# Transposing x by blocks of 32 by 32 on VectorE, with a load that puts the blocks in their places

## The chip, the cores and the metric

The kernel runs on one core of one Trainium2 chip. The time is the device time of one execution in microseconds; of three runs of the kernel before the median is 3130.37 us (3129.48 to 3130.62). All data are float32. The engines of the core are named by their work: TensorE multiplies matrices and writes PSUM (eight banks), VectorE (DVE in the profile) and ScalarE (ACT) work element by element, GpSimd (POOL) issues the gathers and scatters and some sums, and SyncE (SP) only issues DMAs. PEld in the profile is TensorE's weight load, which runs beside the product before it.

## The reference

Four graph layers are applied in turn to `x` of shape 128 x 128 x 256 (graphs, nodes, features); after each one `x = layernorm(x + layer(x))`. Cut to what matters:

```
# layer 0: attention over 512 given edges (src, dst)
Xq, Xv = x @ W_lin.T, x @ W_val.T                    # the products that this change is about
e    = einsum(leaky_relu(Xq[:, src] + Xq[:, dst]), a) + log(adj[src, dst] + 1e-8)
attn = softmax of e over the edges with one src
y    = segment_sum(attn * Xv[:, dst]) @ W_out.T
# layer 1: three times  h = relu((adj * adj) @ (h @ W)), widths 512, 1024, 256 (the last without relu)
# layer 2: diagonal, upper and lower part of adj, each with its own 256 x 256 weight, and a bias
# layer 3: normalized adj @ x, then linear 512, batch norm, relu, linear 256, batch norm
```

Batch norm in layer 3 needs all graphs before it can go on, so the kernel has a main phase and a last phase.

## The kernel before, in words

Four graphs make a quad; there are 32 quads (`NQ`). The 128 nodes lie on the 128 partitions. In the main phase the function `iteration(k)` handles several quads at once, each in another stage: `g = k + 3` is entered (its query and value products, the spill of the queries, the gathers), `e = k + 2` has its edge scores and softmax, `b = k + 1` its aggregation and the first products of layer 1, `c = k` the rest of layer 1 and layer 2, `a = k - 1` layer 3's first half. The order of the work on each engine is the order in which the code calls it; nothing is reordered by a planner (`tc.manual_schedule`). Each engine goes through its own list in order and waits where an operand is not there yet. `start()` and `iteration_0()` bring the first four quads in by hand; quads 4 to 31 go through `iteration(k)` for k = 1 to 28.

The product of layer 0 needs `x` with the features on the partitions. In `iteration(k)` the entering quad goes this way:

- `load_x(g, "xg", 1, xpool)` (lines 203 to 206, called at 945 and for quad 4 at 1089) loads the quad with nodes on the partitions, one DMA on SyncE's queue. There is one buffer `xg`, so the load for the next quad is issued when the last reader of `xg` is done.
- `values_in(g, xg)` (lines 236 to 248) transposes it: for each pair of graphs four products of TensorE with the identity into one PSUM bank (line 245), and a copy by VectorE to a buffer `xt` (line 247).
- `query_sums(g)` (line 318) calls `node_blocks`, which makes four sums of blocks (lines 181 to 184). They serve a product scheme with seven block products in place of eight (class `Seven`, steps `p1` to `p7`).
- `queries(g, room)` (line 298) is that scheme for the query and value weights side by side; its products are on line 289, the kept parts are copied by ScalarE on line 306, and sums with kept parts are on line 314.
- `spill(g)` (line 265) writes the queries to DRAM through SyncE's queue, and `gather(g)` (GpSimd, line 336) reads them back by edge ends, first three gathers by `src`, then three by `dst` that add. `score(g, 0)` (lines 368 to 371, VectorE) reads the first of them.

The order around the change. The large product of layer 1, `second(c, between)`, has 14 places at which other work is slipped in; place 11 takes the transposes (and before them the start of the softmax of `e`), place 12 two scans of that softmax:

```
between[11].append(lambda: next(steps, None))
if has_g:
    between[11] += [lambda: values_in(g, quads[g].xg), lambda: query_sums(g)]
between[12] += [lambda: next(steps, None)] * 2
```

After `second` come, in this order: the load of the next `xg`, `stage_f(a)` (16 products, line 801, and two copies by ScalarE into `ag`, line 804), and then the steps of the query product `q` mixed with those of `h`, layer 3's first linear product (line 837):

```
stage_f(a)
h = hidden(a, room[5:] + room[2:4])
q.p1()
next(steps, None)
run(q.p5, q.p2, q.p6)
run(h.p1, h.p5)
```

`q.p6` adds to the bank that `q.p1` filled, so it waits until ScalarE has kept that bank (line 306). On ScalarE that copy stands behind the last relu of `second` (line 596, which takes a sum that VectorE makes on line 592) and behind the two copies into `ag`.

SyncE's queue carries in each pass, in this order: the load of `xr` (line 205), the store `x3d` (788), the load of `xg` (205), the spill `qd` (268), the store `zd` (858), the load of the attention weights `ad` (427). `node_blocks` is also called by `first_seven` (line 506) on the tiles `mx`.

Of the kernel before, what the change touches and what calls it, by code (L numbers as in the profile page):

```python
# [8 lines left out]
F32 = mybir.dt.float32  # L9
# [17 lines left out]
def gnn_stack(ctx: ExitStack, tc: tile.TileContext, x, adj, w_qv_t, a, w_out_t, src, dst,  # L27
# [14 lines left out]
    nc = tc.nc  # L42
# [86 lines left out]
    with ExitStack() as phase:  # L129
# [73 lines left out]
        def load_x(q, tag="xr", bufs=3, pool=wk):  # L203
            t = pool.tile([P, QB, D], F32, tag=tag, name=f"{tag}{q}", bufs=bufs)
            nc.sync.dma_start(t, x[q * QB:(q + 1) * QB].rearrange("b n d -> n b d"))
            return t

        quads[0].xr = load_x(0)
        wqv = cload([P, DC, 2 * D], "wqv", w_qv_t.rearrange("(c p) f -> p c f", p=P), pool=xpool)
        a_sb = cload([P, N], "adj", adj)  # L210
# [22 lines left out]
        def temp(name):  # L233
            return wk.tile([P, 512], F32, tag="t", name=name, bufs=6)

        def values_in(k, xg, copy=None):

            copy = copy or nc.vector.tensor_copy
            s = quads[k]
            s.xts = []  # L240
            for j in range(0, QB, 2):
                pt = ps("pt").rearrange("p (b c n) -> p b c n", b=2, c=DC)
                for t in range(2):
                    for c in range(DC):
                        nc.tensor.transpose(pt[:, t, c, :], xg[:, j + t, c * P:(c + 1) * P], ident)
                xt = temp("xt").rearrange("p (b c n) -> p b c n", b=2, c=DC)
                copy(xt, pt)
                s.xts.append(xt)
# [28 lines left out]

        def node_blocks(tiles, room):

            a = {f"A{j + 1}{c + 1}": tiles[j][:, :, c, :] for j in range(2) for c in range(2)}  # L280
            for i in range(4):
                a[f"S{i + 1}"] = room[i // 2][:, (i % 2) * 256:(i % 2 + 1) * 256].rearrange("p (b n) -> p b n", b=2)
            sums_a(a, a)
            return a
# [31 lines left out]
            return Seven(node_product(blocks, queries.blocks), part, out)  # L316

        def query_sums(k):
            quads[k].x_blocks = node_blocks(quads[k].xts, [temp("xs") for _ in range(2)])

        def gather(k):

# [179 lines left out]
        def first_seven(k):  # L502

            s = quads[k]
            room = room_of("adc", 4)
            a = node_blocks([s.mx[0], s.mx[2]], room)

            def part(bank, i):

                to = room[2 + i % 2]  # L510
                nc.scalar.copy(to, bank)
                return to

            def out(row, col, bank, kept_):
                h1 = temp("h1")
                if kept_ is not None:
                    nc.vector.tensor_add(h1, bank, kept_)
                nc.scalar.activation(h1, bank if kept_ is None else h1, AF.Relu)
                for t in range(2):
                    for c in range(2):  # L520
                        s.h1[2 * row + t, 2 * col + c] = h1[:, (2 * t + c) * P:(2 * t + c + 1) * P]

            return Seven(node_product(a, first_seven.blocks), part, out)
# [377 lines left out]
        def iteration(k):  # L901
            a, c, b, e, g = k - 1, k, k + 1, k + 2, k + 3
            has_c, has_b, has_e, has_g = c < NQ, b < NQ, e < NQ, g < NQ
            if has_b and b > 2:
                quads[b].xr = load_x(b)
            if has_c:
                late_sums(c)
            parts = quads[a].layer2
            if not has_c:

                h = quads[a - 1].hidden
                h.p6()
                for _ in range(4):
                    next(parts)
                next(parts)
                h.p7()
                for _ in parts:
                    pass

                def amid():  # L920
                    run(h.p4, h.p3)
                    hidden_stats(a - 1)

                stage_f(a, amid)
                for i in range(K3):
                    hidden_last(a, i)
                return
            steps = softmax_parts(e) if has_e else iter(())
            if has_c:
                between = {i: [] for i in range(14)}  # L930
                for i in (0, 1, 2, 3, 5, 7):
                    between[i].append(lambda: next(parts, None))
                between[11].append(lambda: next(steps, None))
                if has_g:
                    between[11] += [lambda: values_in(g, quads[g].xg), lambda: query_sums(g)]
                between[12] += [lambda: next(steps, None)] * 2
                if has_e:
                    for c_, i in enumerate((0, 2, 4)):
                        between[i].append(lambda c_=c_: score(e, c_ + 1))
                if has_b:  # L940
                    for j, i in enumerate((5, 8, 9, 10)):
                        between[i].append(lambda j=j: by_row(b, j))
                second(c, between)
            if has_g and g + 1 < NQ:
                quads[g + 1].xg = load_x(g + 1, "xg", 1, xpool)
            elif has_g:
                kept["w2t"] = xpool.tile([P, K3, D], F32, tag="xg", name="l3w2", bufs=1)
                nc.sync.dma_start(kept["w2t"], l3_w2_t.rearrange("(c p) f -> p c f", p=P))
            if has_c:
                room = room_of("m2", 7)  # L950
            next(steps, None)
            if has_g:
                q = queries(g, room[:3])
            stage_f(a)
            if not has_b:
                last_sums()
                h = quads[a].hidden = hidden(a, room[5:] + room[3:5])
                for _ in third(c, 0):
                    pass
                rest = third(c, 2)  # L960
                next(rest)
                third_mix(c, 0)
                third_norm(c, 0)
                for _ in rest:
                    pass
                h.p1()
                third_mix(c, 2)
                third_norm(c, 2)
                lower = kept["m2"][:, :3 * 512].rearrange("p (t f) -> p t f", t=2)
                quads[c].layer2 = layer2(c, None, lower)  # L970
                next(quads[c].layer2)
                run(h.p5, h.p2)
                next(quads[c].layer2)
                return
# [9 lines that stand above are left out]
                q.p7()  # L984
            run(h.p2, h.p6)
            next(steps, None)
            if has_g:
                run(q.p4, q.p3)
                spill(g)
            h.p7()  # L990
            if has_b:
                aggregate(b)
            run(h.p4, h.p3)
            hidden_stats(a)
            if has_g:
                gather(g)
            if has_b:
                stage_a(b)
            for _ in third(c, 0):
                pass  # L1000
            if has_e:
                attention(e)
                scatter(e)
            rest = third(c, 2)
            mix1(b, 0)
            mix1(b, 2)
            third_mix(c, 0)
            next(rest)
            w = first_seven(b)
            third_norm(c, 0)  # L1010
            next(rest)
            run(w.p1, w.p5, w.p2)
            next(rest)
            if has_g:
                score(g, 0)
                gather_last(g)
            w.p6()
            next(rest, None)
            w.p7()
            third_mix(c, 2)  # L1020
            w.p4()
            w.p3()
            quads[c].layer2 = layer2(c, b)
            next(quads[c].layer2)
            third_norm(c, 2)
            next(quads[c].layer2)
# [56 lines left out]
        def late_loads():  # L1083
            nc.sync.dma_start(w3_sb, w3.rearrange("(c p) f -> p c f", p=P))
            for c in range(DC):
                nc.sync.dma_start(l2w[:, c, :].rearrange("p (k f) -> p k f", k=3),
                                  l2_w[:, c * P:(c + 1) * P, :].rearrange("k p f -> p k f"))
            nc.sync.dma_start(l3w1, l3_w1_t.rearrange("(c p) f -> p c f", p=P))
            quads[4].xg = load_x(4, "xg", 1, xpool)

        def small_loads():
            nc.sync.dma_start(bias, bass.AP(tensor=l2_bias.tensor, offset=l2_bias.offset, ap=[[0, P], [1, D]]))
# [537 lines left out]
```

## Time and profile before

| what | value |
|---|---|
| median of three runs | 3130.37 us |
| profiled execution | 3130.48 us, its span 3128.8 us |
| granted TensorE clock, mean | 0.997 |
| TensorE transposes of `xg` (L245) | 232, 8 a quad, 272 ns each, started 0.11 us apart |
| VectorE copies of them (L247) | 56, 2 a quad, 681 ns each |
| load of `xg` | 29 DMAs of 512 KB, 0.38 us of issue, 3.8 us to landing (median) |
| one pass of `iteration(k)` | 85.74 us |

The profile is of one execution on the chip, taken by the hardware profiler. Each instruction has a start, a length, the engine, the line of the kernel and the names of the tiles. In the order of time, a bracket tells how long the engine was idle before the instruction and what ended that; no bracket means that it followed on. Matmuls are pipelined: the length shown is from start to end of one, while the next one starts earlier, so what a group takes is read from its start to the start of the next group. Times are counted from the start of the span.

### The profile page before, as it was taken

To read this page: it belongs to the slowest core of one execution; us is meant where nothing else is said; L and a number is where in the kernel's file an instruction comes from. 1 tells how busy PE (TensorE), PEld (TensorE's weight loads), DVE (VectorE), ACT (ScalarE), POOL (GpSimd) and SP (SyncE) were. 2 spreads that over 40 slices of the span, in tenths; PEclk is the share of its full clock that TensorE was granted. 3 is DMA by queue.
4 is the path that set the end of the run, shared out by engine and by line. 5 is a ranking of instruction groups with operands and counts; after the bars stand their busy time and mean duration, and the time that the engine had idled before them with its cause. 6 is when DMAs were issued, how large, how long until landed. Compare 5 with 4: busy or idle time off the path is not lost. (4 is left out here: it accounts for less than half of the span.)

```text
span 3128.8 us, 39836 instructions
## 1 busy us (share of the span) xinstructions
PE 3075.6 (98%) x14800; PEld 2401.8 (77%) x14800; DVE 2316.9 (74%) x4600; ACT 1375.8 (44%) x2548; POOL 652.3 (21%) x536
## 2 busy tenths in 40 slices
PE   8899999999999999999999999999999999999987
PEld 4688888888888888888888888888888887874444
DVE  8777777777777777777777777777777776458888
ACT  3344443444444444434344444444443444326668
POOL 3311112222211111122222211111222220001135
PEclk9999999999999999999999999999999999999999
DMA  5633233333333332333333333323333331005557
GB/s 182 160 102 94 77 94 109 99 104 109 108 102 82 108 96 80 89 108 102 102 109 109 102 89 101 97 78 95 104 102 101 109 108 41 21 27 206 176 193 273
DMA packets 117473, 340.05 MB, mean 109 GB/s; under 512 B 14880, under 2 KB 51616, under 8 KB 108960
## 3 DMA queue, kind: packets, MB, share of 16 engines
q0 software_dynamic: 44688, 148.40, 19.4%
q1 hardware_dynamic: 70832, 188.18, 16.9%
q8 instruction: 118, 1.93, 0.3%
q10 hardware_dynamic: 1760, 0.92, 0.1%
q14 instruction: 75, 0.61, 0.1%
HBM read 252.00 MB, written 85.46 MB: 108 GB/s over the span
## 5 line engine op out<-in xcount | busy, mean ns | idle before, releaser
L580 PE MATMUL ph<-m,w 128*128 128x256 f32 x2048 | 473.1, 379 | 0.0
L660 PE MATMUL p<-w,h 128*128 128x256 f32 x2048 | 462.8, 379 | 0.0
L580 PEld LDWEIGHTS ph<-m,w 128*128 128x128 f32 x2048 | 386.8, 190 | 77.9 <-issue 14.8
L660 PEld LDWEIGHTS p<-w,h 128*128 128x128 f32 x2048 | 388.9, 190 | 66.4 <-issue 7.9
L336 POOL DMA_INDIRECT zs<-qd,src_idx x120 | 116.3, 969 | 1372.6 <-DMA qd<-qt 1338.2
L580 PE MATMUL ph<-m,w_s 128*128 128x256 f32 x1536 | 357.7, 379 | 0.4 <-DVE h L592 0.4
L580 PEld LDWEIGHTS ph<-m,w_s 128*128 128x128 f32 x1536 | 291.7, 190 | 53.6 <-issue 14.8
L336 POOL DMA_INDIRECT zs<-qd,dst_idx x120 | 189.0, 1575 | 332.5 <-DMA zs<-qd,src_idx 323.7
L586 ACT COPY u<-ph 128x512 f32<-128x512 f32 x128 | 74.8, 584 | 354.9 <-PE ph L580 354.9
L418 POOL DMA_INDIRECT attd<-at,att_idx x128 | 141.3, 1104 | 340.3 <-DMA attd<-at,att_idx 252.4
L596 ACT ACTIVATE h<-h 128x512 f32<-128x512 f32 x192 | 121.1, 631 | 138.9 <-DVE h L592 138.9
L113 ACT ACTIVATE ln_sd<-ln_mv,eps 128x2 f32<-128x2 f32 x192 | 55.9, 291 | 276.6 <-DVE ln_mv L108 276.6
L368 DVE SCALAR_TENSOR_TENSOR zs<-zs 128x1024 f32<-128x1024 f32 x125 | 151.4, 1211 | 7.1 <-DMA zs<-qd,dst_idx 5.1
L370 DVE TENSOR_TENSOR zs<-zs,a_bc 128x1024 f32<-128x1024 f32 x125 | 153.1, 1225 | 4.3
L371 DVE TENSOR_REDUCE scores<-zs 128x16 f32<-128x1024 f32 x125 | 152.5, 1220 | 4.3
L723 ACT COPY x2k<-y 128x384 f32<-128x384 f32 x192 | 92.0, 479 | 144.5 <-PE y L716 109.9
L106 DVE BATCH_NORM_STATS2 ln_st<-xr 128x6 f32<-128x256 f32 x384 | 144.6, 419 | 6.6
L121 DVE TENSOR_SCALAR xr<-xr,ln_mv,ln_rs 128x256 f32<-128x256 f32 x384 | 142.8, 414 | 7.0
L592 DVE TENSOR_TENSOR h<-ph,u 128x512 f32<-128x512 f32 x128 | 87.0, 680 | 71.7 <-PE ph L580 54.4
L437 ACT COPY adc<-ad 128x512 f32<-128x512 f32 x125 | 132.9, 1065 | 8.6 <-DMA ad<-attd 8.6
L684 POOL TENSOR_TENSOR xb<-xr,bias 128x512 f32<-128x512 f32 x64 | 99.2, 1549 | 150.7 <-DVE xr L121 143.7
L537 PE MATMUL pm<-wt_t,h 128*128 128x128 f32 x1024 | 126.9, 277 | 0.0
(347 smaller groups left out, 6086.3 us busy)
## 6 DMA issues: line engine op xcount, KB each, us to landing
ad<-attd SPq DMA_DIRECT2D x32, 1024.0 KB, 4.8
zd<-z SPq DMA_DIRECT2D x31, 1024.0 KB, 7.4
zl<-zd SPq DMA_DIRECT2D x62, 512.0 KB, 3.8
xr<-in_x_dram SPq DMA_DIRECT2D x32, 512.0 KB, 7.2
x3d<-xr SPq DMA_DIRECT2D x32, 512.0 KB, 2.6
x3l<-x3d SPq DMA_DIRECT2D x32, 512.0 KB, 5.3
out_dram<-x3l POOLq DMA_DIRECT2D x31, 512.0 KB, 5.7
xg<-in_x_dram SPq DMA_DIRECT2D x29, 512.0 KB, 3.8
```

Source lines behind the costliest of these rows:

```text
L106: nc.vector.bn_stats(st[:, i, :], r[:, i, :])
L121: nc.vector.tensor_scalar(r[:, i, :], r[:, i, :], mv[:, i, 0:1], rs[:, i:i + 1], op0=ALU.subtract, op1=ALU.mult)
L336: nc.gpsimd.indirect_dma_start(out=s.z[c], out_offset=None, in_=s.qd, in_offset=bass.IndirectOffsetOnAxis(ap=idx[:, c:c + 1], axis=0), com ...
L368: nc.vector.scalar_tensor_tensor(z, z, SLOPE, z, op0=ALU.mult, op1=ALU.max)
L370: nc.vector.tensor_mul(z3, z3, a_bc.unsqueeze(1).to_broadcast([P, QB, D]))
L371: nc.vector.reduce_sum(s.es[:, c, :], z.rearrange("p (r d) -> p r d", d=DH), axis=AX.X)
L418: nc.gpsimd.indirect_dma_start(out=ad, out_offset=bass.IndirectOffsetOnAxis(ap=att_idx[:, c:c + 1], axis=0), in_=s.at[:, c, :], in_offset= ...
L437: (copy or nc.scalar.copy)(s.adc[:, j * H:(j + 1) * H, :], s.ad.rearrange("p (s r) -> p r s", r=R)[:, j * H:(j + 1) * H, :])
L537: nc.tensor.matmul(pm[:, c // 2, c % 2, :], quads[k].h1[i, c], wt_t, start=True, stop=True)
L580: nc.tensor.matmul(bank[g][:, i].rearrange("p b n -> p (b n)"), wa[:, c, f:f + P], s.m2[:, blk_b, c].rearrange("p b n -> p (b n)"), start= ...
L596: nc.scalar.activation(h, h if src_ is None else src_, AF.Relu)
L660: nc.tensor.matmul(p3[:, t * D:(t + 1) * D], s.h2[f // 2][:, f % 2, j + t, :], w3_sb[:, f, :], start=(f == 0), stop=(f == K2 - 1))
```

## The change

The load of a quad from 4 on is made by `load_turned`: eight DMAs, one for each block of 32 features, each to 32 partitions. Partition i*32 + n of the tile then holds, for feature block i, the nodes n, 32 + n, 64 + n and 96 + n of the four graphs, 32 features each (128 bytes that lie together in DRAM). A VectorE transpose of every 32 by 32 block in place then leaves the features on the partitions and the nodes along the row, one transpose of 128 x 512 for each half of the features. `values_in` is no longer called for these quads; its products with the identity and its copies out of PSUM go away there. The first four quads are brought in as before. `node_blocks` takes the two halves of the features as separate tiles.

```diff
+        B = 32
+
+        def load_turned(q):
+            t = xpool.tile([P, DC, QB * N], F32, tag="xg", name=f"xg{q}", bufs=1)
+            xq = x[q * QB:(q + 1) * QB].rearrange("b (j n) d -> n (b j) d", n=B)
+            for c in range(DC):
+                for i in range(P // B):
+                    d0 = c * P + i * B
+                    nc.sync.dma_start(t[i * B:(i + 1) * B, c, :].rearrange("p (m d) -> p m d", d=B), xq[:, :, d0:d0 + B])
+            return t
...
         def node_blocks(tiles, room):
-            a = {f"A{j + 1}{c + 1}": tiles[j][:, :, c, :] for j in range(2) for c in range(2)}
+            a = {f"A{j + 1}{c + 1}": tiles[j][c] for j in range(2) for c in range(2)}
...
         def query_sums(k):
-            quads[k].x_blocks = node_blocks(quads[k].xts, [temp("xs") for _ in range(2)])
+            s = quads[k]
+            xt = [temp("xt") for _ in range(DC)]
+            for c in range(DC):
+                nc.vector.transpose(xt[c], s.xg[:, c, :])
+            s.x_blocks = node_blocks([[t[:, j * 256:(j + 1) * 256].rearrange("p (b n) -> p b n", b=2) for t in xt]
+                                      for j in range(2)], [temp("xs") for _ in range(2)])
...
-            a = node_blocks([s.mx[0], s.mx[2]], room)
+            a = node_blocks([[s.mx[j][:, :, c, :] for c in range(DC)] for j in (0, 2)], room)
...
                 if has_g:
-                    between[11] += [lambda: values_in(g, quads[g].xg), lambda: query_sums(g)]
+                    between[11].append(lambda: query_sums(g))
...
-                quads[g + 1].xg = load_x(g + 1, "xg", 1, xpool)
+                quads[g + 1].xg = load_turned(g + 1)
...
-            quads[4].xg = load_x(4, "xg", 1, xpool)
+            quads[4].xg = load_turned(4)
```

## The prediction

> **What bounds the kernel now.** I read the page first (busy shares), then the busy time of each engine over one pass of the steady loop, then in order of time the instructions of TensorE, VectorE and ScalarE around the edited place, the waits, and last the SyncE queue and the DMA rows. The first line is the page's, the second the busy time by stretch (length, then PE, PEld, DVE, ACT, POOL with counts, granted clock, DMA share, GB/s).
>
> ```profile
> PE 3075.6 (98%) x14800; PEld 2401.8 (77%) x14800; DVE 2316.9 (74%) x4600; ACT 1375.8 (44%) x2548; POOL 652.3 (21%) x536
> ...
> 1055.35:1141.09 85.74, 85.74 (x435) 70.63 (x434) 63.67 (x125) 35.80 (x67) 16.86 (x14) 1.00 0.35 99
> ```
>
> One pass takes 85.74 us, TensorE is busy in all of it at the full granted clock, VectorE in 63.67. So a TensorE instruction that goes should shorten the pass, unless something else at that very place is as late as TensorE is. That is the question here, so the order of time (start, length, engine, line):
>
> ```profile
> 1055.24 0.27 PE L385 MATMUL pe<-ident,scores 128*128 128x128 f32 x1
> 1055.35 1.04 PE L245 MATMUL pt<-ident,xg 128*128 128x128 f32 x8
> 1056.23 1.89 PE L580 MATMUL ph<-m,w 128*128 128x256 f32 x8
> ...
> 1063.20 1.03 PE L289 MATMUL x<-wqv,xt 128*128 128x256 f32 x4
> 1064.06 1.11 PE L289 MATMUL y<-wqv_s,xs 128*128 128x256 f32 x4
> 1065.00 1.03 PE L837 MATMUL y<-ag,l3w 128*128 128x256 f32 x4
> ```
>
> ```profile
> 1055.45 0.69 DVE L592 TENSOR_TENSOR h<-ph,u 128x512 f32<-128x512 f32 x1 [1.39 <-PE ph L580]
> 1056.05 1.28 DVE L247 COPY xt<-pt 128x512 f32<-128x512 f32 x2
> 1057.37 0.42 DVE L181 TENSOR_TENSOR xs<-xt 128x256 f32<-128x256 f32 x1
> ...
> 1061.22 0.65 DVE L592 TENSOR_TENSOR h<-ph,u 128x512 f32<-128x512 f32 x1
> ```
>
> ```profile
> 1061.91 0.63 ACT L596 ACTIVATE h<-h 128x512 f32<-128x512 f32 x1 [2.63 <-DVE h L592]
> 1062.44 1.05 ACT L804 COPY ag<-pa 128x512 f32<-128x512 f32 x2
> 1063.38 0.60 ACT L306 COPY m<-y 128x512 f32<-128x512 f32 x1
> ```
>
> ```profile
> PEld y L289 <- ACT m L306: 6.0, 28, 0.2
> ```
>
> The reader is to see a second chain beside TensorE's own. VectorE waits for a product until 1055.45 and then runs with no idle bracket: the sum L592, the two copies of the edit, four node sums, two scans, the next L592, done at 1061.87. ScalarE's relu L596 waits 2.63 us for exactly that; behind it in ScalarE's order stand the two `ag` copies and the copy L306, which ends at 1063.98. Step p6 of the query product (y<-wqv_s,xs at 1064.06) cannot begin before it: the last line says that its weight load waits for L306 in all 28 passes, 0.2 us each, and its group is 1.11 us long where its neighbours are 1.03. So at 1064 the two chains arrive together. TensorE has no slack there, and neither has the way over VectorE and ScalarE.
>
> **The change, part by part.**
>
> *Removed on TensorE.* 8 transposes a quad for quads 4 to 31, 28 quads (the first four still go through the identity). The group starts at 1055.35 and the next at 1056.23; start to start it is 0.873 us in the median of the 28 groups, 24.45 us in all. Sent through in full, this is 3130.48 - 24.45 = 3106.0. But TensorE would be at p6 at 1063.19, while L306 ends at 1063.98: VectorE's start at 1055.45 hangs on a product ahead of the transposes, and none of its work down to L592 was waiting for TensorE. So what is late next is L306, and the 0.87 us becomes a wait before p6. Taken at 0 us, if VectorE's part keeps its length.
>
> *Exchanged on VectorE.* Two copies out of PSUM, 1056.05 to 1057.37, 1.32 us with the step to L181, become two transposes of 128x512. No transpose of VectorE is in the trace. By rows of its other work: two 128x512 operations within SBUF follow each other at 0.72 us when the first is not overlapped (L553 at 1116.73, L554 at 1117.45), so 1.44 us, which is +0.12 us a quad. If the operation goes at half that rate, it is like a 128x1024 row (L368 to L370, 1.25 us apart): 2.50 us, +1.18 us. At a quarter, 5.0 us, +3.7 us. At twice the rate it is like the 128x256 sums, 0.34 to 0.46 us apart: 0.8 us, -0.52 us. I take +0.12, since operations on 512 elements within SBUF (L553, 682 ns) and out of PSUM (L247, 681 ns) agree and are the nearest. Every such difference goes 1:1 through L592, L596, L804 and L306 into p6 and so into the pass, since no engine idles between: 28 x 0.12 = +3.4 us.
>
> The page "VectorE: DVE Perf Modes" of the Trainium skill, section "The three transpose paths", gives 311 ns for a 128x128 transpose in bf16; with 384 more columns at the page's 0.96 GHz an estimate is 711 ns, and the sum would be 3133 instead. The same section warns that a plain DMA with a transposing access pattern is 19 times slower than the crossbar's 1309 ns; were that so here, 8 blocks would take some 199 us a quad and no pass could hide it. Its condition is a large stride of the innermost run at the destination, which these loads do not have; no row of this trace shows such a load.
>
> *Added waits on VectorE.* The transposes read what eight DMAs wrote, four each. The nearest row is L412, which waits for the landings of four scatters with two semaphore instructions of 50 ns a pass. They pass while the operation ahead (L592, 0.69 us) still runs: 0 us; without that cover 4 x 0.05 us, 28 x 0.2 = 5.6 us. Queued behind are the node sums, the scans and L592. The node sums read 256 elements as before, 0 us.
>
> *The load.* One DMA of 512 KB (512 runs of 1 KB) becomes eight, with 4096 runs of 128 bytes.
>
> ```profile
> 1056.42 0.38 SPq L205 DMA_DIRECT2D xg<-in_x_dram  x1
> 1071.00 0.32 SPq L268 DMA_DIRECT2D qd<-qt  x1
> ...
> L1095 SPq DMA_DIRECT2D bn<-in_l_g_dram x2: 868/951/1034, 116.1 to 118.7; - x2
> ```
>
> ```profile
> 1058.50:1059.00 0.50, 0.50 (x4) 0.45 (x3) 0.50 (x3) 0.50 (x2) 0.00 (x0) 1.00 1.08 385
> ...
> 121.75:122.25 0.50, 0.50 (x5) 0.42 (x4) 0.00 (x0) 0.41 (x1) 0.50 (x1) 1.00 0.38 3
> ```
>
> In the first stretch only xg moves: 385 GB/s for 0.5 us are 188 runs of 1 KB, 1.08 x 16 x 0.5 us of engine time, 46 ns each. In the second only the runs of 4 bytes of `bn` move: about 375 in 3.0 us, 8 ns each. So 128 bytes cost between 8 and 46 ns, 256 runs an engine 2 to 12 us. Issuing 512 small runs took 0.48 to 1.03 us on the SyncE queue (L1095), eight of them 4 to 8 us, and at the 2.53 us of the worst `bn` row 20 us. I take 8 us. The first issue waits for the second transpose (1057.4) where it waited for the last product (1056.42). It ends near 1066 and the spill `qd<-qt`, next on the queue, goes at 1071. In use is the tile a pass later, near 1142. Both at 0 us. The cover beyond: if the spill is late, so are the gathers; the first `dst` gather is issued at 1078.42 and lands in 7.4 us (the median), after 1.6 us of issuing near 1087, and score L368 reads it at 1096.23. So 9 us more are free, and the load may last 22 us, 85 ns a run.
>
> "DMA: Bandwidth & Descriptors", section "Specifications", says that under 512 bytes a transfer is read, modified and written, which speaks against the change. With the page's 32 bytes a beat, 3 beats of overhead and 850 MHz a run of 128 bytes is 8.2 ns by estimate, 16 if done twice, 4 us a load: the sum would stay. No row here has runs of 128 bytes.
>
> *The load of quad 4*, at 96.84, stands where the DMA engines are full (share 1.06 from 96 to 104, 0.32 to 106) and the scatter issued at 102.65 starts a chain by which TensorE idles 3.77 us at 130.27. More small runs delay it by 0 to 4 us: I take 0.5, as 256 runs at 13 ns (estimated between the two rows) are 3.3 us of an engine against 1.5 now. *Two PSUM banks a quad* fewer: no wait for a bank is in the waits there, 0 us.
>
> **Sum.** -24.45 + 24.45 (wait before p6) + 3.4 + 0.5 = +3.9 us on the profiled execution's 3130.48 us (span 3128.8 and 1.7 around it), which stands 0.1 over the median: 3134 us.
>
> **Rivals.**
> - *The gain comes through in part (faster):* VectorE's transposes are shorter than the copies. At -0.52 us a quad it is 14.6 us: 3116. For it: nothing is read from PSUM any more. Against: L553 and L247 agree. It decides from 0.54 us a transpose (0.66 a copy now), where 28 x 0.24 = 6.8 us, less the 0.5 of the start, passes 0.2%.
> - *A slow transpose (slower):* half rate, +1.18 us a quad, +33: 3164. A quarter: +104, 3235. For it: 4-byte elements, no row. It is outside 0.2% from +0.21 us a quad (28 x 0.21 + 0.5 = 6.4).
> - *Small transfers are costly:* at the 142 ns a run of xg's start (share 0.32 and 37 GB/s from 1057.5 to 1058, some 18 runs in 2.6 us), a load takes 36 us, the spill lands 23 us late, 14 us after what L368 can spare: 28 x 14 = 392, with nothing gained: 3520. Against: the 46 and 8 ns.
> - *GpSimd meets VectorE:* in five passes a node sum (L182 at 335.14) lasts 2.66 us instead of 0.29 beside GpSimd's L684 and TensorE loses 0.8 us. Other phases could make that all 28: 23 x 0.85 = +20, 3154.
>
> **How the numbers follow.** Forecast 0.55, its own range 3129 to 3140 (VectorE from 0 to +0.3 a quad, semaphores and start included). Partial gain 0.12, half rate 0.13, quarter 0.04, costly small transfers 0.08, meeting 0.08. 0.2% is 6.3 us, about what a measurement here can tell from no change. Of the forecast 0.34 lies within it, 0.19 above, 0.02 below. Faster 0.14, same 0.34, slower 0.52. The range goes from the partial gain to the half rate, 3114 to 3165, and leaves out the quarter, the costly transfers and a rest of the first: under 0.15.
>
> **What would show it.** Right: no L245 on `xg`; VectorE's transposes near 0.7 us; a new wait of some 0.8 us of PEld for ACT m L306 in 28 passes; the spill no later after p2 than now; a pass of 85.8 to 86.0 us. Wrong: L306 no longer waited for, with a pass near 84.9 (I misread the chain); transposes over 1 us; SyncE or GpSimd's gathers late and L368 waiting.

## The result and the profile after

The changed kernel takes 3131.11 us (median of four runs, 3128.98 to 3131.60) against 3129.93 us before (median of four). The ratio is 1.0003, its 95% interval 0.9985 to 1.0020: no difference that can be measured. The profiled execution took 3130.88 us with a span of 3129.2, against 3130.48 and 3128.8 before. The difference of 0.40 us is itself a sum: the last of the scores' products (L404, L385 before) starts 1.65 us earlier than before, 0.8 us of it from before the first pass and 1.2 because GpSimd lengthens a node sum of VectorE in four passes and not in five; the last phase, which the edit does not touch, lasts 2.05 us longer. The work did change as the diff says: on the page TensorE has 14576 products where it had 14800 (28 quads times 8), and no transposes of `xg` by TensorE are left but those of quad 3.

```profile
PE 3058.4 (98%) x14576; PEld 2378.8 (76%) x14576; DVE 2316.7 (74%) x4600; ACT 1374.4 (44%) x2548; POOL 652.9 (21%) x536
```

TensorE is busy 17 us less (3075.6 before), in a span of the same length: it has started to wait. The busy time by stretch over one pass of the changed kernel (length, then PE, PEld, DVE, ACT, POOL with counts, clock, DMA share, GB/s):

```profile
1054.60:1140.35 85.75, 85.05 (x427) 69.75 (x426) 63.38 (x127) 35.77 (x67) 17.02 (x14) 1.00 0.37 99
```

The pass is 85.75 us where it was 85.74, but TensorE now stands idle for 0.70 us of it. Where, the order of time on TensorE shows (start, length, engine, line; the bracket is idle time and what ended it):

```profile
1053.77 0.27 PE L404 MATMUL pe<-ident,scores 128*128 128x128 f32 x1
1053.88 1.89 PE L599 MATMUL ph<-m,w 128*128 128x256 f32 x8
...
1060.85 1.03 PE L302 MATMUL x<-wqv,xt 128*128 128x256 f32 x4
1062.58 1.13 PE L302 MATMUL y<-wqv_s,xs 128*128 128x256 f32 x4 [0.70 <-ACT m L319]
```

The large product follows the scores directly (0.11 us from start to start); the 0.87 us of transposes between them are gone. The next change in the rhythm is p6: it starts 1.73 us after the group before it, where one group takes 0.866. VectorE and ScalarE over the same time:

```profile
1053.97 0.69 DVE L611 TENSOR_TENSOR h<-ph,u 128x512 f32<-128x512 f32 x1 [1.41 <-PE ph L599]
1054.58 1.29 DVE L336 STREAM_TRANSPOSE xt<-xg 128x512 f32<-128x512 f32 x2
1055.90 0.43 DVE L181 TENSOR_TENSOR xs<-xt 128x256 f32<-128x256 f32 x1
...
1057.38 1.21 DVE L408 TENSOR_TENSOR_SCAN m<-reset_f,pair 16x512 f32<-16x512 bf16 x1
1058.62 1.21 DVE L410 TENSOR_TENSOR_SCAN m<-reset_b,m 16x512 f32<-16x512 bf16 x1
1059.76 0.65 DVE L611 TENSOR_TENSOR h<-ph,u 128x512 f32<-128x512 f32 x1
```

```profile
1060.44 0.63 ACT L615 ACTIVATE h<-h 128x512 f32<-128x512 f32 x1 [3.03 <-DVE h L611]
1060.98 1.05 ACT L823 COPY ag<-pa 128x512 f32<-128x512 f32 x2
1061.92 0.60 ACT L319 COPY m<-y 128x512 f32<-128x512 f32 x1
```

The two transposes stand where the two copies stood, and take as long: 1.32 us with the step to L181, before and after. So the chain from L611 over L615 and L823 to the kept copy L319 has kept its length (1053.97 to 1062.52 is 8.55 us; before, 1055.45 to 1063.98 was 8.53). TensorE's own way to p6 has become 0.87 us shorter, and it waits for the difference. The relu L615 waits 3.03 us for VectorE where its predecessor waited 2.63. The waits of the changed kernel (total, times, longest) say that this is so in all 28 passes:

```profile
PEld y L302 <- ACT m L319: 30.9, 28, 1.1
PE y L302 <- ACT m L319: 19.6, 28, 0.7
```

The load goes out as eight DMAs, and its queue is free again long before the spill `qd<-qt` (SyncE of the changed kernel, and the transposes and the load's DMAs of the whole execution: shortest, median and longest issue or instruction in ns):

```profile
1055.90 4.05 SPq L218 DMA_DIRECT2D xg<-in_x_dram  x8
1069.53 0.34 SPq L281 DMA_DIRECT2D qd<-qt  x1
```

```profile
L218 SPq DMA_DIRECT2D xg<-in_x_dram x224: 312/487/2122, 95.8 to 2433.1; - x112
L336 DVE STREAM_TRANSPOSE xt<-xg x56: 668/686/703, 195.8 to 2514.8; 128x512 f32<-128x512 f32 x56
```

The spill goes 15.76 us behind the scores' product L404, as before. The execution's 114688 runs of 128 bytes took 12.7 ns each in the packet records.

### The profile page after: what moved, and what is told of

Read it like the earlier page. It is cut to its first block, busy times and chain, and to the rows that moved or that the text cites. A ratio compares the mean times of both kernels' runs of the same rounds, so it can differ in the third digit from the quotient of the medians.

```text
span 3129.2 us, 39724 instructions
## 1 busy us (share of the span) xinstructions
PE 3058.4 (98%) x14576; PEld 2378.8 (76%) x14576; DVE 2316.7 (74%) x4600; ACT 1374.4 (44%) x2548; POOL 652.9 (21%) x536
## 5 line engine op out<-in xcount | busy, mean ns | idle before, releaser
L615 ACT ACTIVATE h<-h 128x512 f32<-128x512 f32 x192 | 121.1, 631 | 150.1 <-DVE h L611 150.1
L611 DVE TENSOR_TENSOR h<-ph,u 128x512 f32<-128x512 f32 x128 | 86.9, 679 | 72.0 <-PE ph L599 54.7
```

The source lines that it names most:

```text
L615: nc.scalar.activation(h, h if src_ is None else src_, AF.Relu)
```

## The experiments

**The theory.** A chain over VectorE and ScalarE reaches p6 at the same time as TensorE's own work did; it runs through two softmax scans (L408, L410) that stand between the transposes and the sum L611 and that nobody at p6 needs. The change shortens TensorE's way alone, so it is worth nothing until the chain is shorter too. The rivals: the gain is eaten by the load (SyncE, DMA engines), or something else sets the pass.

Two kernels move the scans behind L611, in the changed kernel and in the kernel before:

```diff
-                between[12] += [lambda: next(steps, None)] * 2
+                between[13] += [lambda: next(steps, None)] * 2
```

> The changed kernel with the two softmax scans moved from place 12 to place 13 of the large product, that is behind VectorE's last sum for ScalarE's relu. Theory (the gain is kept back by the chain VectorE sum, transposes, node sums, two scans, sum, then ScalarE's relu, two ag copies and the kept copy, then step p6): the chain is 2.4 us shorter, the wait before p6 of 0.86 us a pass goes, 28 passes give 24 us: 3106 to 3109 us, and a pass is 84.9 us. Rival 1 (the load in small runs costs what the transposes gave back): the scans have nothing to do with it, 3131. Rival 2 (TensorE's transposes cost nothing before, as they ran in a gap): 3131.

> The kernel before with the same move of the two scans. Theory: before the change TensorE and the chain arrive at p6 together, only 0.08 us a pass are lost there, so the move alone gives 28 x 0.08 = 2 us: 3128. Rival (the place of the scans is worth something by itself, whatever transposes): as much as the move gives on the changed kernel, 3106.

The changed kernel with the scans moved takes 3104.46 us (3102.45 to 3105.49), against the kernel before on the same chip 0.9922 (0.9906 to 0.9939): faster. The kernel before with the scans moved takes 3126.49 us, 0.9991 (0.9982 to 1.0001): hardly anything. Both are as the theory said, each some 1.5 us under what was expected. The pass in the traces is 85.74 us before, 85.75 with the change, 85.66 with the scans moved alone, and 84.78 with both. In the kernel with both, TensorE is busy for the whole pass, and p6 follows in its rhythm, 0.86 us after the group before it:

```profile
1043.31:1128.09 84.78, 84.78 (x427) 69.83 (x426) 63.41 (x125) 35.94 (x67) 17.03 (x14) 1.00 0.37 100
```

```profile
1050.28 1.03 PE L302 MATMUL x<-wqv,xt 128*128 128x256 f32 x4
1051.14 1.03 PE L302 MATMUL y<-wqv_s,xs 128*128 128x256 f32 x4
```

On VectorE the sum now goes ahead of the scans, and in the kernel before with the scans moved p6 follows in the same rhythm (VectorE with both edits, then TensorE with the move alone):

```profile
1046.97 0.69 DVE L611 TENSOR_TENSOR h<-ph,u 128x512 f32<-128x512 f32 x1
1047.57 1.20 DVE L408 TENSOR_TENSOR_SCAN m<-reset_f,pair 16x512 f32<-16x512 bf16 x1
```

```profile
1061.21 1.03 PE L289 MATMUL x<-wqv,xt 128*128 128x256 f32 x4
1062.07 1.03 PE L289 MATMUL y<-wqv_s,xs 128*128 128x256 f32 x4
```

With both edits ScalarE now waits for TensorE before the kept copy (0.24 us) and not the other way round; what waits for the scans is only the exponential's table load behind it:

```profile
1049.62 0.58 ACT L319 COPY m<-y 128x512 f32<-128x512 f32 x1 [0.24 <-PE y L302]
1050.81 1.28 ACT L415 ACT_TABLE_LOAD   x1 [0.61 <-DVE pair L413]
```

So the transposes are worth 0.88 us a pass (85.66 to 84.78) as soon as the chain does not stand in the way; the move is worth 0.08 us without the change and 0.97 with it. Neither part gives what the two give together. The kernel with both is the fastest of this study.

**p6 moved behind another step.** If only the wait at p6 stands in the way, a step put ahead of p6 should cover it. TensorE does `h.p1` first:

```diff
-                run(q.p5, q.p2, q.p6)
-            run(h.p1, h.p5)
+                run(q.p5, q.p2)
+            h.p1()
+            if has_g:
+                q.p6()
+            h.p5()
```

> The changed kernel with TensorE's order alone changed: step p1 of the hidden product (0.87 us) goes ahead of step p6 of the query product; VectorE and ScalarE keep their lists. Theory: TensorE comes to the hidden step 0.86 us before p6 could start, waits some 0.4 us for the second ag copy, and the kept copy is ready when it comes to p6: 0.3 to 0.6 us a pass gained, 3114 to 3122 us. Rival (the time is lost in the load or anywhere else than in front of p6): 3131.

This missed: 3143.06 us, 1.0046 (1.0030 to 1.0063), slower. The wait before p6 is gone but for 0.24 us of its weight load, and a longer one has come two steps on, before p7 (TensorE, then ScalarE):

```profile
1066.04 1.03 PE L856 MATMUL y<-ag,l3w 128*128 128x256 f32 x4
1066.90 1.13 PE L302 MATMUL y<-wqv_s,xs 128*128 128x256 f32 x4
1067.87 1.03 PE L856 MATMUL z<-ag,l3w_s 128*128 128x256 f32 x4
1069.79 1.13 PE L302 MATMUL y<-wqv_s,xs 128*128 128x256 f32 x4 [0.89 <-ACT m L319]
```

```profile
1066.87 1.28 ACT L415 ACT_TABLE_LOAD   x1
1068.16 0.63 ACT L415 ACTIVATE pair<-pair 16x512 f32<-16x512 f32 x1
1068.70 0.56 ACT L860 COPY m<-y 128x512 f32<-128x512 f32 x1
1069.16 0.57 ACT L319 COPY m<-y 128x512 f32<-128x512 f32 x1
```

The expectation took it that ScalarE keeps its list, and it does not: the code calls the copy of a bank together with the product that fills it (`p1` and `p6` of `Seven`), so the edit changes ScalarE's order too. With p6 behind `h.p1`, the copy of `h`'s bank (L860) has come ahead of the copy of p6's bank (L319), and both stand behind the table load and the exponential, 1.83 us from 1066.87 to 1068.70, which ScalarE begins as soon as the late first L319 is done. p7 needs the second L319. The pass is 86.05 us: 0.30 more than with the change as it is, 28 x 0.30 = 8.4 us of the 11.7 between the spans; another 2.6 us come from seven passes, where it had been four, in which GpSimd meets a node sum of VectorE. The expectation had looked at one meeting of the two chains, and there are two.

**One transpose more a pass.** Is the chain really stretched one to one by what VectorE does there, and what is a transpose worth? The kernel repeats the second transpose of each quad.

```diff
                 nc.vector.transpose(xt[c], s.xg[:, c, :])
+            nc.vector.transpose(xt[1], s.xg[:, 1, :])
```

> The changed kernel with one transpose of VectorE a pass made a second time (the second half into the same buffer). Theory: VectorE's part is on the chain that sets p6, so 0.6 to 0.75 us more there are 0.6 to 0.75 us a pass, 28 passes 17 to 21 us: 3148 to 3152 us. Rival (VectorE has 20 us of slack in a pass and TensorE alone is the bound): 3131.

Measured: 3149.58 us, 1.0064 (1.0047 to 1.0081). The pass grows from 85.75 to 86.50, which is what the third transpose takes on VectorE to the step after it (1062.52 to 1063.26), and the wait before p6 grows from 0.70 to 1.45:

```profile
1061.19 1.29 DVE L336 STREAM_TRANSPOSE xt<-xg 128x512 f32<-128x512 f32 x2
1062.52 0.71 DVE L337 STREAM_TRANSPOSE xt<-xg 128x512 f32<-128x512 f32 x1
1063.26 0.43 DVE L181 TENSOR_TENSOR xs<-xt 128x256 f32<-128x256 f32 x1
```

28 x 0.75 are 21 us; the spans differ by 19.1. The 28 passes together are 21.8 us longer, with one more meeting of GpSimd and a node sum, and the last phase, which the edit does not touch, is 1.9 us shorter in this execution. In the changed kernel a time on VectorE between the two L611 is paid in full.

**The same transpose with the scans moved.** After the miss with p6 the room was read at both meetings, from the trace with the scans moved alone.

> The kernel with the scans moved behind the sum L611, and beside that one transpose of 128x512 more on VectorE in every pass (a repeat of the second, which changes nothing in what is computed). In the trace with the scans moved alone, L319 ends at 1050.20 and p6 starts at 1051.14, so p6 would bear some 1.1 us more on VectorE (0.94, and 0.24 in which L319 waits for TensorE). The extra transpose took 0.75 us a pass where the scans stood ahead. p7 has less room: its own kept copy, behind the exponential, ends at 1053.20 and p7 starts at 1053.73, 0.53 us. So theory (only what reaches a kept copy before TensorE does counts): no wait before p6, a wait of 0.15 to 0.25 us before p7 in 28 passes, +4 to +7 us over 3104.5, that is 3108 to 3112. Rival (VectorE's work counts in full wherever it stands): +21, 3125. Second rival (all of it is free here): 3104.

Measured: 3109.16 us, 0.9935 (0.9918 to 0.9951), and a pass of 85.00 us, 0.22 over the 84.78. There is no wait before p6. The waits (total, times, longest) and TensorE at p7, which starts 0.97 us behind the group before it and not 0.86:

```profile
PEld y L302 <- ACT m L319: 9.7, 28, 0.3
```

```profile
1057.40 1.03 PE L857 MATMUL z<-ag,l3w_s 128*128 128x256 f32 x4
1058.37 1.13 PE L302 MATMUL y<-wqv_s,xs 128*128 128x256 f32 x4
```

The same instruction costs 21 us in one order (28 x 0.75) and 6 in the other (28 x 0.22; the medians differ by 4.7, and by 6.4 if each is taken against the kernel before on its own chip, 3130.10 and 3128.43). The 0.22 arise where the room was 0.53 us, at p7, not at p6, where it was 1.18, and they are the transpose's 0.75 less that room. With that the explanation of the run with p6 moved has also been tried by a prediction and not only read from its trace.

**The load.** Three kernels vary it. The first loads the quad in one DMA of 1 KB runs:

```diff
-            xq = x[q * QB:(q + 1) * QB].rearrange("b (j n) d -> n (b j) d", n=B)
...
+            nc.sync.dma_start(t.rearrange("p c (b d) -> p (c b) d", d=D), x[q * QB:(q + 1) * QB].rearrange("b n d -> n b d"))
```

> The changed kernel with its load in one DMA of 1 KB runs again, as before the change; it leaves out the placing of the blocks, so the transposes take x in the wrong order. Theory (the load is hidden: its issue of 4 us and its 5.5 us of transfer stand beside work that does not wait for it): 3131, pass 85.75, the same 0.87 us lost before p6. Rival (the gain is eaten by the small runs, through SyncE or through the DMA engines): 3106, pass 84.9. At quad 4 the load's issue took 10 us of SyncE against one issue; if that delays the scatter there, up to 1 us less at the start.

Measured: 3129.33 us, 1.0002 (0.9992 to 1.0011), pass 85.75 us, the same 0.70 us of idle time before p6. The eight DMAs and the small runs cost nothing that can be seen, and taking them away brings nothing. The rival that the load eats the gain is out.

The other two cut the runs to 32 and to 16 bytes, in 32 and 64 DMAs a quad (here 32; for 16 bytes 4 stands for 8):

```diff
+                    for s in range(0, B, 8):
+                        nc.sync.dma_start(t[i * B:(i + 1) * B, c, :].rearrange("p (m d) -> p m d", d=B)[:, :, s:s + 8],
+                                          xq[:, :, d0 + s:d0 + s + 8])
```

> The load in 32 DMAs a quad with runs of 32 bytes, 512 runs each. By the 0.49 us that one issue of 512 runs took, SyncE is busy for 16 us from 1055.9, so the spill goes near 1072 and not at 1069.5, some 3 us late, and 16384 runs at the 12.7 ns measured for 128 bytes take 13 us on 16 engines. Theory (9 us of the spill's delay are free before a score waits): pass 85.75, 3131, and up to 20 us more at quad 4 alone, where the eight issues already took 10 us. Rival (no slack behind the spill): 3 us a pass, 3215. If a run of 32 bytes costs four times less than one of 128, nothing changes in this sum, since the issue sets it.

> The load in 64 DMAs a quad with runs of 16 bytes. SyncE is busy for 31 to 32 us from 1055.9, the spill goes near 1087 and not at 1069.5, 18 us late. Theory (9 us of it are free): the pass grows by some 9 us, 28 x 9 = 250, and the start by up to 40: 3380 to 3430, with the scores waiting for the gathers. Rival (the issue itself is not what costs, the queue runs ahead of the engines): 3131 to 3160. Rival (no slack at all): 28 x 18, 3640.

With 32 bytes: 3134.39 us, 1.0017 (1.0007 to 1.0027). The pass stays at 85.76 us although SyncE is busy with the load for 17.9 us and, in the pass shown, the spill goes 11.46 us behind p6, where it went 6.95 behind:

```profile
1065.29 17.89 SPq L219 DMA_DIRECT2D xg<-in_x_dram  x32
1083.43 0.34 SPq L283 DMA_DIRECT2D qd<-qt  x1
```

The few us more are made once, at quad 4, where the load holds SyncE for 27.9 us and the attention weights behind it come late: the first step of the aggregation on TensorE starts 67.8 us after the same step of the quad before it, and 56.6 us in the kernel with the change. Of these 11.3 us 1.7 are made up in the pass after and 3.1 over the 28 passes, in which GpSimd meets no node sum in this execution; the last phase is 1.7 us shorter, for no reason that the trace shows. The spans differ by 5.5 us.

With 16 bytes: 3510.14 us, 1.1211 (1.1192 to 1.1230), 80 us over the expectation's upper end. The pass is 98.79 us. SyncE, VectorE and TensorE of that kernel:

```profile
1119.21 35.01 SPq L219 DMA_DIRECT2D xg<-in_x_dram  x64
1154.47 0.34 SPq L283 DMA_DIRECT2D qd<-qt  x1
```

```profile
1170.48 1.22 DVE L389 SCALAR_TENSOR_TENSOR zs<-zs 128x1024 f32<-128x1024 f32 x1 [12.08 <-DMA zs<-qd,dst_idx]
```

```profile
1174.87 2.08 PE L304 MATMUL z<-w,adc 128*128 128x256 f32 x4 [10.22 <-DVE h L538]
```

The way is the expected one: the spill is late (28.34 us behind p6, 21.4 more than with the change as it is), so the gathers are, the score waits for the last of them, and TensorE waits for the sum L538 behind the score. The free part is then 21.4 - 10.2, some 11 us, where 9 were reckoned. Two sizes were off. The 64 issues took 35.0 us and not 31 or 32, since in such a row one takes 0.55 us and not the median 0.49. And the wait has an after-effect: the product behind it takes 2.08 us where such a group takes 1.03. The busy time by stretch, around the same wait one pass earlier (TensorE is idle from 1065.9 to 1076.3), gives the granted clock (third last column):

```profile
1066.00:1076.20 10.20, 0.00 (x0) 0.00 (x0) 4.26 (x5) 0.00 (x0) 4.13 (x3) 0.73 0.91 182
...
1078.00:1079.00 1.00, 1.00 (x6) 0.86 (x5) 0.62 (x1) 0.00 (x0) 0.23 (x1) 0.50 0.04 8
...
1080.00:1081.00 1.00, 1.00 (x8) 1.00 (x6) 0.53 (x3) 0.40 (x2) 0.63 (x1) 0.57 0.00 0
1081.00:1083.00 2.00, 2.00 (x21) 2.00 (x19) 1.97 (x8) 0.00 (x0) 0.96 (x1) 1.00 0.02 4
```

The clock falls during the idle time, by the mean of 0.73 some 4.7 us after its start, and by the row with 0.57 it stays at half until 1080.9, some 4.6 us into the work after it. From the end of the wait to the first product of layer 2 (L737) TensorE needs 7.7 us in the median of the passes, where the changed kernel needs 5.4: 2.3 us are lost on top of each wait. So 10.2 + 2.3 + 0.24 (p6's own wait, 0.94 for 0.70) make most of the 13.04 us by which the pass has grown. The start adds its part, as expected: the step that came 67.8 us after its predecessor above comes after 91.6. The Trainium skill, page "TensorE: Matmul & The Clock Gate", section "What's actually happening", says of this gate: half speed after an idle window of about 3.4 us, full speed after about as long a stretch of work. The rows agree in kind, and both stretches measured here are longer (4.7 and 4.6 us); in the changed kernel, whose wait at p6 is 0.70 us, the clock over the pass is 1.00.

## Why the prediction was right, point by point

The forecast was 3134 us, its own range 3129 to 3140; measured 3131.11. The sum has +3.9 us on the profiled execution; the two profiled executions differ by +0.40. That this is so near to nothing is in part luck: the last phase (+2.05 us), the time before the first pass (-0.8) and GpSimd's meetings (-1.2) nearly cancel, and the sum had 0.5 for the start alone. The pass, 85.75 us for 85.74, does not hang on them.

1. *The removed transposes against the wait before p6, 0 us:* right, and shown by more than the sum. The copy that the changed kernel waits for is the one named, in 28 passes, PEld for 1.1 us (0.8 was said), the pass is the same to 0.01 us, and moving the scans, which shortens that chain alone, releases 0.97 us a pass. Without the change the same move releases 0.08.
2. *VectorE's exchange, +0.12 us a quad, +3.4 us:* this term was too large. The transposes take 686 ns in the median (681 had been read for the copies), and from the first to L181 it is 1.327 us for 1.314: +0.01 a quad, some 0.4 us in all. What failed is the row chosen for the step. L553 and L554 follow each other at 0.72 us and are not overlapped, and L554 reads the block that L553 has just written; the two transposes are overlapped, as the two copies were, 0.625 us from start to start against 0.598. They read and write different halves and tiles. In the run with a third transpose the repeat writes the tile just written, and the step to it is 0.70; from the last transpose to the sum L181, which reads its tile, it is 0.70 with two transposes and 0.75 with three. That such a difference goes into the pass in full was right: +0.75 us on VectorE gave +0.75 a pass. Beside the measured 686 ns the Trainium skill, page "VectorE: DVE Perf Modes", section "The three transpose paths", had led to an estimate of 711; its warning of strided DMA loads does not meet this load, as the next point shows.
3. *The load, 0 us:* right. The issue took 4.05 us, the lower end of 4 to 8; 8 had been taken. A run took 12.7 ns, between the 8 and 46 of the bounds. The cover was reckoned at 9 us behind the spill; it is at least some 4.5 (32 bytes, nothing lost in the pass) and about 11 (16 bytes).
4. *Quad 4, +0.5 us:* not there. The load held SyncE for 10 us, but TensorE's idle time at 129.46 is 3.69 us, 3.77 before; it waits for scores and not for the load. From 32 DMAs on there is an effect.
5. *Added waits of the transposes, PSUM banks, 0 us:* nothing speaks against them. The transposes follow L611 with no idle time, and the exchange leaves some 0.4 us in all.
6. *The rivals.* Partial gain: it needed a transpose under 0.54 us, and it takes 0.69. Half and quarter rate: out by the same row. Costly small transfers: out at 128 bytes; the price of 3520 us is nearly reached with runs of 16 bytes (3510), and by 64 issues, not by slow runs, for a run of 16 bytes took 8.6 ns and the DMA engines were busy for half of the 35 us. GpSimd meeting a node sum: it did so in four passes (0.7 to 0.95 us more in each) where it had been five, and not in all 28.

The point reckoned least well was one the prediction didn't need: it knew one meeting of the two chains, p6, and spoke as if the pass would be 84.9 once L306 was not waited for. The run with p6 moved showed the second meeting, p7.

## What to carry to other kernels

Work taken off the busiest engine is worth what the other way to the next meeting lets through: follow the order of time from the removed instruction to the first step that waits for another engine, see whether that engine's own chain ends there at the same time, and if it does, look in that chain for work that the step doesn't need. Here the 24 us of removed transposes came through only when two scans were moved behind the sum; alone, each of the two edits gave nothing measurable. Before a step is moved, look at every place where the two chains meet, since engines go through their lists in order and a copy that changes its place can be late at the next one.

## What the runs showed of the hardware that was not expected

- A VectorE transpose of 128 x 512 floats by blocks of 32 costs what a copy of the same size out of PSUM costs, 686 and 681 ns. The next one started 0.625 us after it where it wrote another tile, and 0.70 where it wrote the same one.
- Small runs were cheap on the DMA engines: 128 bytes took 12.7 ns, 32 and 16 bytes both 8.6 ns, 1 KB 46 ns (median). The page "DMA: Bandwidth & Descriptors" of the Trainium skill, section "Specifications", speaks of a read, change and write under 512 bytes; by its figures 128 bytes were estimated at 8.2 ns, or 16 if done twice, and the measured time lies between; whether such a read and write back takes place no run here shows. What the small runs did cost was the issue, about half a microsecond for each DMA of 512 runs (4.05 us for 8, 17.9 for 32, 35.0 for 64).
- A wait of TensorE of 10 us costs some 2.3 us more than itself: after 27 such waits in the run with 16 bytes (8 to 12 us) the granted clock was at half for the next 3.2 to 6.2 us of work.
